# Seven block products for the second product of experts 3 to 6, and scatters of one expert that do not wait for one another

## The chip, the cores and the metric

The kernel runs on one core of a Trainium2 chip. The core has five engines with queues of their own: PE (TensorE, matrix products; its weight loads are listed apart as PEld), DVE (VectorE), ACT (ScalarE), POOL (GpSimd, which also issues the indirect DMAs) and SP (SyncE, which only issues DMAs here). Each engine works through its own instructions in order and waits on semaphores for the others. The time is that of one execution on the device in microseconds (us); the figure given is the median of several.

## The reference, cut to what matters

The whole network is four layers on 4096 tokens of width 256, all in 32-bit floats: a gated attention layer, a low-rank feed-forward layer, a 16-head attention with relu weights, and a mixture of experts. The change is in the last one:

```python
S = sigmoid(xt @ Wg).T              # 8 experts x 4096 tokens
G, I = top_k(S, 1024)               # each expert takes its 1024 best tokens
ex = xt[I]                          # gathered rows
hid = gelu(einsum('ekh,ehf->ekf', ex, W1) + b1)       # 256 -> 1024
out = (einsum('ekf,efh->ekh', hid, W2) + b2) * G      # 1024 -> 256
new_x = zeros_like(xt).at[I].add(out)                 # scattered back, added
```

Then `new_x` is normalized by rows and added to `x`. The tokens of one expert are distinct; two experts may take the same token, so a row of `new_x` may be added to by several experts.

## The kernel before, in words

Experts are worked on one after another, 0 to 7 (`e`). An expert's 1024 tokens are two units of 512 (`u = 2e` and `2e + 1`, `q` is 0 or 1), each of four tiles of 128 tokens.

*Lists.* For each expert a threshold is searched and the list of its tokens is built by small steps on DVE, PE and ACT (`sort`, `rank`, `chunks`, `places`, `collect`, `gather`). These steps stand in an agenda, and `go_on_with_lists(u, time)` (L2357), called after pieces of the main work, takes the next step when the time credited since the last one suffices and the step is due at unit `u`. The list of expert `e` is due from unit 2e - 3 on, its gather from 2e - 2. The gather (L2003 to L2012) is eight indirect DMAs issued by POOL that fetch rows of tokens into `got`.

*Turning.* `turn` (L2167) transposes four tiles of gathered rows on PE into a PSUM bank and copies them to `xT`, the layout that the first product wants. `turns_within` (L2209) says after which tile of the second product of the expert before this is done.

*First product.* Experts 0, 1, 2 and 7 use `feed_forward` (L2275). Experts 3 to 6 use `feed_forward_by_seven` (L2225): a 2 x 2 block product in the form of Winograd, with seven block products in place of eight. Its token sums T1, T2, T3, T4 are made on DVE (`token_sums`, L2202), its weight sums S1 to S4 on POOL (`weight_sums`, L2190). For each of four `f` it makes seven matmuls of 128 x 512 into four PSUM banks a, b, c, d, adds them up on DVE and applies gelu on ACT into `hid`.

*Second product.* `project_back` (L2307): for each tile of 128 tokens, eight matmuls (one for each 128 of the 1024 hidden features) of 256 columns accumulate in one PSUM tile `py` (tag "y", two buffers). DVE adds the bias (L2331) and multiplies by the gates (L2332) into `y`, and POOL adds the rows to `acc_d` in memory by an indirect DMA with addition (L2333). The hidden block is the stationary operand (128 x 128), the weights `w2` are the moving one.

*Order of scatters.* Every scatter writes `acc_d`, so each waits until the one before has landed. For expert 6 alone they are declared independent of one another (L2342 to L2344); they are collected in `summed`.

*Expert 7.* Its result is not scattered. When expert 6's scatters have landed, SP reads blocks of 512 rows of `acc_d` back (`read_back`, L2053) and POOL fetches the rows of expert 7's own tokens (`fetch_acc`, L2084). Then, between the matmuls of expert 7, the steps of `beside_last` (L2134) run: statistics of a block on DVE and POOL (`all_stats`), scaling on ACT (`all_scaled`), addition to the output (`all_out`, on POOL's queue for blocks 0 to 4, DVE and SP for 5 to 7), and the same for expert 7's own rows (`known`, `chosen_stats`, `chosen_less_mean`, `chosen_sum`, `chosen_out`). Keys such as `(0, "f", 6)` mean: in unit q = 0, after feature block 6 of the first product; `"i"` means after tile i of the second.

*What sets the order.* PE, DVE and ACT run in the order in which the program is written (`manual_schedule`). POOL's order is planned by the framework's scheduler up to expert 5, and is the written one from expert 6 on (L2391). SP issues loads in order. PSUM has eight banks: one for `parts`, five with tag "mm", two for tag "y"; a tag's buffers are used in turn, and one that is used again waits until its last reader is done.

Of the kernel before, what the change touches and what calls it, by code (L numbers as in the profile page):

```python
# [9 lines left out]
F32 = mybir.dt.float32  # L10
# [4 lines left out]
ALU = mybir.AluOpType  # L15
# [4 lines left out]
P = 128  # L20
# [54 lines left out]
def kernel(  # L75
# [1679 lines left out]
    with ExitStack() as st4:  # L1755
# [364 lines left out]
        def begin_last():  # L2120
# [45 lines left out]

        def turn(u, c, half=None):  # L2167

# [3 lines left out]
            tiles = range(NJ) if half is None else range(half * NJ // 2, (half + 1) * NJ // 2)  # L2172
            tp = ps.tile([P, NJ, P], F32, tag="mm", name="tp", bufs=5)
            for i in tiles:
# [34 lines left out]
        def turns_within(u):  # L2209

            e, q = divmod(u, QPE)
            if u == QPE * NE - 1:
                return {}
            turns = {c: (lambda c=c: turn(u + 1, c)) for c in range(DC)}
            if q == QPE - 1 and by_seven(e + 1):
                both = [
                    turns[0], turns[1], lambda: turn(u + 2, 0), lambda: token_sums(e + 1, 0), lambda: turn(u + 2, 1),
                    *(lambda n=n: token_sums(e + 1, n) for n in (1, 2, 3)),
                ]
                return {0: both[0:1], 1: both[1:4], 2: both[4:]}  # L2220
            if by_seven(e) and q == 0:
                return {}
            return {2: [turns[0], turns[1]]} if u == 1 else {1: [turns[0]], 2: [turns[1]]}

        def feed_forward_by_seven(e):  # L2225
# [81 lines left out]
        def project_back(u, hid):  # L2307
# [4 lines left out]
            for i in range(NJ):  # L2312
                k = q * NJ + i
                py = ps.tile([P, D], F32, tag="y", name="py")
                for f in range(FC):
# [14 lines left out]
                y = wk.tile([P, D], F32, tag="y", name="y", bufs=7)  # L2330
                nc.vector.tensor_tensor(y, py, mb2[:, e, :], ALU.add)  # L2331
# [102 lines left out]
```

## Time and profile before

| | |
|---|---|
| median of 3 runs | 1458.32 us (1456.48 to 1459.18) |
| profiled execution | 1456.37 us, of which the span from first to last instruction is 1454.2 us |
| PE busy in the span | 1405.7 us, 97% |
| DVE, ACT, POOL busy | 869.7, 735.8, 531.7 us |
| granted PE clock | 0.985 of full, on average |
| expert 3 starts (first matmul of its first product) | 1169.2 us |
| experts 4, 5, 6, 7 start | 1224.2, 1279.3, 1334.3, 1388.4 us |
| last matmul | about 1444 us |

A row of the chain of work reads: start, length, engine, output tile, line, and how many records it merges. A 32-bit matmul leaves two records. A row of the timeline of one engine reads: start, length, engine, line, operation, output <- input, shape; in brackets the idle time of that engine before it and what ended it. A row of the table by stage reads: start:end, length, and for PE, PEld, DVE, ACT and POOL the busy time with the number of instructions, then the granted PE clock, the DMA share and GB/s.

### The profile page before, as it was taken

Reading aid. Unit: us, or ns where it says so; the run is one execution under the profiler, and the core shown is the slowest. Engines: PE = TensorE matmul, PEld = TensorE weight load, DVE = VectorE, ACT = ScalarE, POOL = GpSimd, SP = SyncE. Lnnn points to the kernel's source line nnn. Section 1 sums busy time; section 2 is a strip of 40 time slices with the busy share of each in tenths; the row PEclk is TensorE's granted clock in tenths of the full one; section 3 lists DMA queues with packets and bytes.
Section 4 is the critical chain, followed back from the end, with each engine's and each line's share of the span. In section 5 each row is a group of like instructions: output and inputs, shape, how many; then the busy total and the mean of one; then the engine's idle time right before and its main releaser. Section 6 shows DMA issues by size and latency. Waiting matters only on the chain.

```text
span 1454.2 us, 26447 instructions
## 1 busy us (share of the span) xinstructions
PE 1405.7 (97%) x10392; PEld 858.6 (59%) x10392; DVE 869.7 (60%) x2133; ACT 735.8 (51%) x1014; POOL 531.7 (37%) x662
## 2 busy tenths in 40 slices
PE   8999999999889999999999999949999999999997
PEld 4666666666644444454444547727666657757774
DVE  5457555666554637664767496885545766365346
ACT  4244454454358887877787888712122131231243
POOL 4123322322352223422333323413425325543765
PEclk9999999999999999999999999979999999999999
DMA  8400000001652473437344721151414233343364
GB/s 223 142 1 1 0 1 1 1 1 38 203 173 76 122 209 104 143 118 232 91 133 144 229 70 39 39 170 38 106 19 127 51 79 70 78 103 62 81 166 134
DMA packets 104853, 138.76 MB, mean 95 GB/s; under 512 B 25469, under 2 KB 64794, under 8 KB 104602
## 3 DMA queue, kind: packets, MB, share of 16 engines
q1 hardware_dynamic: 74512, 81.75, 18.1%
q0 software_dynamic: 30160, 55.32, 16.1%
q8 instruction: 81, 1.33, 0.4%
q14 instruction: 42, 0.34, 0.1%
q10 hardware_dynamic: 58, 0.01, 0.0%
HBM read 75.29 MB, written 61.51 MB: 94 GB/s over the span
## 4 chain that ended last, share of the span: by engine, by line
PE 87%; DVE 5%; issue 3%; POOL 2%; DMA 1%; ACT 1%; SPq 0%; POOLq 0%; ACTq 0%; DVEq 0%
PE po L1553 16%; PE py L2316 14%; PE sc L1532 10%; PE ph L2290 7%; PE ph L2236 7%; PE pg L722 4%; PE pv L738 4%; PE py L848 3%; PE pt L1308 2%; PE pq L397 2%; PE po L820 2%; PE ph L904 2%; PE pv L431 2%; PE po L824 1%; PE pkv L835 1%
## 5 line engine op out<-in xcount | busy, mean ns | idle before, releaser
L1710 ACT ACTIVATE w<-sc 128x1024 f32<-128x1024 f32 x395 | 379.9, 1023 | 60.7 <-PE sc L1532 60.2
L1553 PE MATMUL po<-w,vaug 128*17 128x256 f32 (+1 forms) x4608 | 256.0, 358 | 1.5 <-DVE turned L1611 1.2
L2316 PE MATMUL py<-w,hid 128*128 128x256 f32 x1024 | 228.6, 380 | 0.0
L2316 PEld LDWEIGHTS py<-w,hid 128*128 128x128 f32 x1024 | 191.9, 190 | 29.6 <-issue 4.2
L1712 DVE TENSOR_SCALAR w<-sc 128x1024 f32<-128x1024 f32 x117 | 142.4, 1220 | 79.4 <-PE sc L1532 75.9
L1553 PEld LDWEIGHTS po<-w,vaug 128*17 128x17 f32 x4608 | 116.3, 97 | 117.9 <-issue 48.2
L1532 PE MATMUL sc<-q,kT 64*128 64x512 f32 (+1 forms) x1152 | 170.3, 403 | 2.5 <-ACT w L1710 1.3
L2333 POOL DMA_INDIRECT acc_d<-y,idx x56 | 88.6, 1583 | 163.0 <-issue 38.6
L1532 PEld LDWEIGHTS sc<-q,kT 64*128 64x128 f32 x1152 | 90.1, 185 | 83.5 <-issue 46.6
L2297 ACT ACTIVATE hid<-ph,mb 128x512 f32<-128x512 f32 (+1 forms) x72 | 46.0, 639 | 159.6 <-PE ph L2290 133.3
L2290 PE MATMUL ph<-xT,w 128*128 128x512 f32 (+1 forms) x288 | 114.8, 552 | 0.3 <-DVE xT L2181 0.3
L2005 POOL DMA_INDIRECT got<-tok_d,idx x64 | 66.6, 1040 | 72.1 <-DVE idx L1995 54.1
L2290 PEld LDWEIGHTS ph<-xT,w 128*128 128x128 f32 x288 | 52.6, 190 | 51.3 <-issue 48.3
L371 POOL DMA_DIRECT2D kT<-k_d x32 | 23.4, 732 | 118.0 <-PE sc L1532 54.0
L722 PE MATMUL pg<-nT,wh 128*128 128x512 f32 x128 | 61.6, 613 | 1.5 <-ACT nT L661 1.5
L2331 DVE TENSOR_TENSOR y<-py,mb 128x256 f32<-128x256 f32 x56 | 23.5, 420 | 64.3 <-PE py L2316 54.9
L848 PE MATMUL py<-wo,oT 128*128 128x256 f32 x256 | 61.6, 384 | 0.0
L738 PE MATMUL pv<-wh,nT 128*128 128x512 f32 x128 | 59.7, 593 | 0.0
L848 PEld LDWEIGHTS py<-wo,oT 128*128 128x128 f32 x256 | 47.5, 190 | 17.6 <-issue 11.1
L746 ACT ACTIVATE v<-v 128x512 f32<-128x512 f32 x32 | 20.2, 630 | 62.7 <-DVE v L745 62.7
L1137 POOL TENSOR_TENSOR rsb<-veb,mhalf 128x1 f32<-128x1 f32 x30 | 19.6, 654 | 86.8 <-DVE veb L1136 86.8
L586 POOL TENSOR_TENSOR x<-x,y 128x1024 f32<-128x1024 f32 x13 | 30.6, 2357 | 56.3 <-ACT y L575 56.3
(352 smaller groups left out, 2344.8 us busy)
## 6 DMA issues: line engine op xcount, KB each, us to landing
q<-q_d POOLq DMA_DIRECT2D x16, 1024.0 KB, 6.0
kT<-k_d POOLq DMA_DIRECT2D x32, 512.0 KB, 8.1
w<-in_L_ffn_W_dram SPq DMA_DIRECT2D x16, 1024.0 KB
k_d<-parts SPq DMA_DIRECT2D x48, 256.0 KB
q_d<-parts SPq DMA_DIRECT2D x48, 256.0 KB
acc_d<-logits SPq DMA_DIRECT2D x8, 512.0 KB
tok_d<-hg SPq DMA_DIRECT2D x30, 128.0 KB
x<-in_L_attn_x_dram SPq DMA_DIRECT2D x7, 512.0 KB
```

Source lines behind the costliest of these rows:

```text
L722: nc.tensor.matmul(pg, lhsT=wh[:, c, HID + e * P : HID + (e + 1) * P], rhs=d["nT"][:, c, :], start=(c == 0), stop=(c == DC - 1),)
L738: nc.tensor.matmul(pv, lhsT=d["nT"][:, c, i * P : (i + 1) * P], rhs=wh[:, c, 0:HID], start=(c == 0), stop=(c == DC - 1),)
L848: nc.tensor.matmul(py, lhsT=d["oT"][:, e, :], rhs=wo[:, e, :], start=(e == 0), stop=(e == EC - 1))
L1532: nc.tensor.matmul(sc[:, j, m * n : (m + 1) * n], lhsT=row["kT"][t, r][rows, u, (kt + m) * P : (kt + m + 1) * P], rhs=row["q"][qh, t][rows ...
L1553: nc.tensor.matmul(po[rows : rows + HD + 1, at : at + n], lhsT=row["v"][:, kt + m, HQ * t + 4 * r + 2 * u + j, :], rhs=w[:, j, (2 * m + pa ...
L1710: nc.scalar.activation(w, sc, AF.Relu)
L1712: nc.vector.tensor_scalar(w, sc, 0.0, None, ALU.max)
L2005: return nc.gpsimd.indirect_dma_start(out=dst, out_offset=None, in_=rows[:, :], in_offset=self.at_chunk(c), bounds_check=NT - 1, oob_is_er ...
L2236: nc.tensor.matmul(bank, lhsT=a[:, f * P : (f + 1) * P], rhs=b, start=start, stop=stop, skip_group_check=not start)
L2290: nc.tensor.matmul(ph, lhsT=w1[:, c, f * P : (f + 1) * P], rhs=xT[u][:, c, h * n : (h + 1) * n], start=(c == 0), stop=(c == DC - 1),)
L2316: nc.tensor.matmul(py, lhsT=hid[:, f, i * P : (i + 1) * P], rhs=w2[:, f, :], start=(f == 0), stop=(f == FC - 1),)
L2333: scatter = nc.gpsimd.indirect_dma_start(out=acc_d[:, :], out_offset=lists[e].at_chunk(k), in_=y, in_offset=None, bounds_check=NT - 1, oob ...
```

## The change

It has four parts.

1. The second product of experts 3 to 6 no longer goes through `project_back` but through a new function, `project_back_by_seven`. The hidden activations (1024 tokens x 1024 features) are cut in 2 x 2 blocks of 512 x 512, the weights in 2 x 2 blocks of 512 x 128. Four weight sums are made on POOL (`back_sums`, emitted after the first `f` of the first product), four sums of hidden blocks on DVE, and seven block products of 16 matmuls each (128 columns) replace the eight. Rooms of weights that are no longer used (`wq1`, `wk1`, `wv`, `wop`) and `accg` hold the sums; the others are made in place. The bias times the gate is written by ACT, the gated sums are added on DVE by blocks of 128 x 128. All eight scatters of an expert come after the sixth and seventh block product.
2. The scatters of one expert are declared independent of one another for every expert, and each waits for all scatters of the expert before.
3. Within experts 3 to 6 the transposes for the next expert use the PSUM tag "y", which the new second product leaves free; `py` tiles become a whole bank each, and `y` gets nine buffers in place of seven.
4. In expert 7 the statistics of the blocks move one step later.

```diff
+        scattered = [*([] for _ in range(NE - 2)), summed]
...
         beside_last = {
-            (0, "f", 5): [(all_stats, 0)],
-            (0, "f", 6): [(all_stats, 1)],
-            (0, "f", 7): [(all_scaled, 0), (known, 0), (all_stats, 2), (fetch_acc, 4, 5)],
-            (0, "i", 0): [(all_out, 0), (all_scaled, 1), (known, 1), (all_stats, 3)],
-            (0, "i", 1): [(all_out, 1), (all_scaled, 2), (known, 2), (all_stats, 4), (fetch_acc, 6, 7)],
-            (0, "i", 2): [(all_out, 2), (all_scaled, 3), (known, 3)],
-            (0, "i", 3): [(all_out, 3), (all_scaled, 4), (all_stats, 5)],
-            (1, "f", 0): [(all_out, 4)],
+            (0, "f", 6): [(all_stats, 0)],
+            (0, "f", 7): [(all_stats, 1), (all_scaled, 0), (known, 0), (fetch_acc, 4, 5)],
+            (0, "i", 0): [(all_out, 0), (all_scaled, 1), (known, 1), (all_stats, 2)],
+            (0, "i", 1): [(all_out, 1), (all_scaled, 2), (known, 2), (all_stats, 3), (fetch_acc, 6, 7)],
+            (0, "i", 2): [(all_out, 2), (all_scaled, 3), (known, 3), (all_stats, 4)],
+            (0, "i", 3): [(all_out, 3), (all_scaled, 4)],
+            (1, "f", 0): [(all_out, 4), (all_stats, 5)],
...
+        def turn(u, c, half=None, tag="mm"):
...
+            tp = ps.tile([P, NJ, P], F32, tag=tag, name="tp", bufs=5 if tag == "mm" else 2)
...
+            tag = "y" if by_seven(e) else "mm"
...
+                if f == 0:
+                    back_sums(e, gelus[-1])
                 go_on_with_lists(QPE * e, 3.0)
-            for q in range(QPE):
-                if q == 0 and by_seven(e + 1):
-                    weight_sums(e + 1, gelus[-1])
-                if q == 0 and e == NE - 2:
-                    fetch_last()
-                project_back(QPE * e + q, hid[q])
+            if by_seven(e + 1):
+                weight_sums(e + 1, gelus[-1])
+            if e == NE - 2:
+                fetch_last()
+            project_back_by_seven(e, hid)
...
+        def back_sums(e, behind):
+            (b11, b12), (b21, b22) = back_blocks(e)
+            t1, t2, t4 = (room.rearrange("p (f n) -> p f n", n=P) for room in back_rooms[:3])
+            for dst, x, y in ((t1, b12, b11), (t2, b22, t1), (b12, b22, b12), (t4, b21, t2)):
+                after_all(nc.gpsimd.tensor_tensor(dst, x, y, ALU.subtract), [behind])
...
+            def product(bank, a, b, start, stop):
+                for i in range(NJ):
+                    for f in range(HC):
+                        nc.tensor.matmul(
+                            bank[:, i * P : (i + 1) * P],
+                            lhsT=a[:, f, i * P : (i + 1) * P],
+                            rhs=b[:, f, :],
...
+            def of_bias(q):
+                for k in range(q * NJ, (q + 1) * NJ):
+                    ys[k] = wk.tile([P, D], F32, tag="y", name="y", bufs=9)
+                    nc.scalar.activation(ys[k], mb2[:, e, :], AF.Identity, scale=gates[k])
+            def add(q, n, src):
+                for i in range(NJ):
+                    k = q * NJ + i
+                    y = ys[k][:, n * P : (n + 1) * P]
+                    nc.vector.scalar_tensor_tensor(y, src[:, i * P : (i + 1) * P], gates[k], y, ALU.mult, ALU.add)
+            def put(q):
+                for k in range(q * NJ, (q + 1) * NJ):
+                    scatter = nc.gpsimd.indirect_dma_start(
...
+                    after_all(scatter, scattered[e - 1] if e else ())
+                    beside_each_other(scatter, scattered[e])
...
+            p1 = new_bank("p1")
+            product(p1, a11, b11, True, True)
+            nc.scalar.copy(u2, p1)
+            nc.vector.tensor_tensor(s1, a21, a22, plus)
+            nc.vector.tensor_tensor(s3, a11, a21, sub)
+            go_on_with_lists(QPE * e, 1.2)
+            p4 = new_bank("p4")
+            product(p4, a22, t4, True, True)
+            nc.vector.tensor_tensor(s2, s1, a11, sub)
+            go_on_with_lists(QPE * e, 1.2)
+            product(p1, a12, b21, False, True)
+            of_bias(0)
+            add(0, 0, p1)
+            nc.vector.tensor_tensor(s4, a12, s2, sub)
+            go_on_with_lists(QPE * e, 1.2)
+            for do in ahead.get(0, ()):
+                do()
+            p5 = new_bank("p5")
+            product(p5, s1, t1, True, True)
+            nc.scalar.copy(kept, p5)
+            for do in ahead.get(1, ()):
+                do()
+            go_on_with_lists(QPE * e + 1, 1.2)
+            p6 = new_bank("p6")
+            product(p6, s2, t2, True, True)
+            nc.vector.tensor_tensor(u2, u2, p6, plus)
+            of_bias(1)
+            for do in ahead.get(2, ()):
+                do()
+            go_on_with_lists(QPE * e + 1, 1.2)
+            p7 = new_bank("p7")
+            product(p7, s3, t3, True, True)
+            nc.vector.tensor_tensor(v, u2, p7, plus)
+            nc.vector.tensor_tensor(c21, v, p4, plus)
+            nc.vector.tensor_tensor(v, v, kept, plus)
+            add(1, 0, c21)
+            add(1, 1, v)
+            put(1)
+            go_on_with_lists(QPE * e + 1, 1.2)
+            product(p5, s4, b22, False, True)
+            nc.vector.tensor_tensor(u2, u2, p5, plus)
+            add(0, 1, u2)
+            put(0)
+            go_on_with_lists(QPE * e + 1, 1.2)
...
-                if e == NE - 2:
-                    beside_each_other(scatter, summed)
+                after_all(scatter, scattered[e - 1] if e else ())
+                beside_each_other(scatter, scattered[e])
```

In `project_back_by_seven`, `a11`, `a12` are the two feature halves of the first unit's hidden block and `a21`, `a22` those of the second; `s1` is a room of its own (`accg`), `s2`, `s3`, `s4` overwrite `a11`, `a21`, `a12`.

More of the change, by code (lines that the diff above doesn't have):

```diff
@@ L2165 @@
         xT = {}
-        def turn(u, c, half=None):
+        def turn(u, c, half=None, tag="mm"):
             if c == 0 and not half:
@@ L2172, in turn @@
             tiles = range(NJ) if half is None else range(half * NJ // 2, (half + 1) * NJ // 2)
-            tp = ps.tile([P, NJ, P], F32, tag="mm", name="tp", bufs=5)
+            tp = ps.tile([P, NJ, P], F32, tag=tag, name="tp", bufs=5 if tag == "mm" else 2)
             for i in tiles:
@@ L2213, in turns_within @@
                 return {}
-            turns = {c: (lambda c=c: turn(u + 1, c)) for c in range(DC)}
+            tag = "y" if by_seven(e) else "mm"
+            turns = {c: (lambda c=c: turn(u + 1, c, tag=tag)) for c in range(DC)}
             if q == QPE - 1 and by_seven(e + 1):
                 both = [
-                    turns[0], turns[1], lambda: turn(u + 2, 0), lambda: token_sums(e + 1, 0), lambda: turn(u + 2, 1),
+                    turns[0], turns[1], lambda: turn(u + 2, 0, tag=tag), lambda: token_sums(e + 1, 0),
+                    lambda: turn(u + 2, 1, tag=tag),
                     *(lambda n=n: token_sums(e + 1, n) for n in (1, 2, 3)),
@@ new lines, in feed_forward_by_seven, with back_blocks @@
+            project_back_by_seven(e, hid)
+        back_rooms = [x.rearrange("p c d -> p (c d)") for x in (wq1, wk1, wv, wop)]
+        def back_blocks(e):
+            w2 = weights[e][1]
+            return [[w2[:, h * FC // 2 : (h + 1) * FC // 2, n * P : (n + 1) * P] for n in range(2)] for h in range(2)]
+        def back_sums(e, behind):
[3 more added lines that the diff above has]
+                after_all(nc.gpsimd.tensor_tensor(dst, x, y, ALU.subtract), [behind])
@@ new lines, in project_back_by_seven, with new_bank @@
+        def project_back_by_seven(e, hid):
+            (b11, t3), (b21, b22) = back_blocks(e)
+            t1, t2, t4 = (room.rearrange("p (f n) -> p f n", n=P) for room in back_rooms[:3])
+            HC = FC // 2
+            (a11, a12), (a21, a22) = ([hid[q][:, h * HC : (h + 1) * HC, :] for h in range(2)] for q in range(QPE))
+            s1 = accg.rearrange("p k d -> p (k d)").rearrange("p (f t) -> p f t", t=TB)
+            s2, s3, s4 = a11, a21, a12
+            u2, v, c21 = back_rooms[3], seven["sum1"], seven["sum0"]
+            ahead = turns_within(QPE * e + 1)
+            gates = [lists[e].got[k][:, D + e : D + e + 1] for k in range(NC)]
+            ys = {}
+            kept = wk.tile([P, TB], F32, tag="kept_back", name="kept_back", bufs=1)
+            def new_bank(name):
+                return ps.tile([P, TB], F32, tag="mm", name=name, bufs=5)
+            def product(bank, a, b, start, stop):
[5 more added lines that the diff above has]
+                            rhs=b[:, f, :],
+                            start=start and not i and not f,
+                            stop=stop and f == HC - 1,
+                            skip_group_check=True,
+                        )
+            def of_bias(q):
[10 more added lines that the diff above has]
+                    scatter = nc.gpsimd.indirect_dma_start(
+                        out=acc_d[:, :],
+                        out_offset=lists[e].at_chunk(k),
+                        in_=ys[k],
+                        in_offset=None,
+                        bounds_check=NT - 1,
+                        oob_is_err=True,
+                        compute_op=ALU.add,
+                    )
+                    after_all(scatter, scattered[e - 1] if e else ())
+                    beside_each_other(scatter, scattered[e])
+            sub, plus = ALU.subtract, ALU.add
+            p1 = new_bank("p1")
[42 more added lines that the diff above has]
+            go_on_with_lists(QPE * e + 1, 1.2)
@@ L2313, in project_back @@
                 k = q * NJ + i
-                py = ps.tile([P, D], F32, tag="y", name="py")
+                py = ps.tile([P, TB], F32, tag="y", name="py")[:, 0:D]
                 for f in range(FC):
@@ L2329, in project_back @@
                     continue
-                y = wk.tile([P, D], F32, tag="y", name="y", bufs=7)
+                y = wk.tile([P, D], F32, tag="y", name="y", bufs=9)
                 nc.vector.tensor_tensor(y, py, mb2[:, e, :], ALU.add)
```

## The prediction

> **What bounds the kernel now.** I read the page's head first, then engine busy time cut by stage, then the chain that ended last inside the expert stage.
>
> ```profile
> span 1454.2 us, 26447 instructions
> PE 1405.7 (97%) x10392; PEld 858.6 (59%) x10392; DVE 869.7 (60%) x2133; ACT 735.8 (51%) x1014; POOL 531.7 (37%) x662
> ...
> 1224.20:1279.30 55.10, 55.10 (x237) 37.33 (x236) 28.72 (x61) 15.41 (x25) 26.66 (x22) 1.00 0.37 80
> ...
> 1388.40:1454.20 65.80, 55.93 (x200) 36.89 (x198) 38.01 (x140) 26.57 (x48) 37.61 (x43) 0.96 0.61 164
> ```
>
> The first row below the dots is expert 4 (start, end, length; then busy us of PE, PEld, DVE, ACT, POOL; granted clock; DMA). PE is busy for all 55.10 us at full clock, so in experts 3 to 6 time is PE time. The last row is expert 7 with the finish: 56 of 65.8 us are PE, and what follows the last matmul is fixed. The chain through expert 4's second product shows no other engine:
>
> ```profile
> 1249.77 17.27 PE py L2316 x80
> 1267.03 0.44 PE tp L2175 x4
> 1267.47 3.46 PE py L2316 x16
> 1270.92 0.87 PE tp L2175 x8
> 1271.80 0.06 PE parts L1907 x2
> 1271.86 3.54 PE py L2316 x16
> 1275.39 0.44 PE tp L2175 x4
> 1275.83 3.46 PE py L2316 x16
> ```
>
> A matmul is two records, so 128 records are 64 matmuls of 256 columns: 17.27 + 3.46 + 3.54 + 3.46 = 27.73 us, 0.433 each. There is no wait in it to spare.
>
> **Product: 64 matmuls of 256 columns become 7 x 16 = 112 of 128 columns.** Such a shape runs in the first layer, eight in a row in the chain:
>
> ```profile
> 79.87 0.22 PE po L820 x2
> 80.09 0.22 PE po L824 x2
> ...
> 81.43 0.22 PE po L824 x2
> 81.66 0.89 PE psim L688 x8
> ```
>
> 81.66 - 79.87 = 1.79 us for eight, 0.224 each: 3.58 per block product, 25.06 per expert, 2.67 less than now, **10.7 us less for four experts**. Half of 0.433 would give 24.3 and 13.9 saved; I take the row, since the shape is the same.
>
> Here a rule speaks against the change. The same row's weight loads take 192 ns each (224 of them) but are busy 34.0 us together, not 43: they overlap one another. The Trainium skill, "TensorE: Matmul & The Clock Gate", section "Back-to-back issue gap", says that in a stream of weight load and matmul pairs both set the spacing: 81 ns for 128 columns against 56 for the matmul alone. That ratio on 0.217 gives 0.314 per matmul, 35.2 us per expert, 7.4 more than now. The eight in the trace keep their pace, so I stay with 0.224 (0.217 to 0.235 for a run of 112).
>
> **Order within an expert.** From T, the end of the first product, PE does p1 to T+3.6, p4 to 7.2, p1's second half to 10.7, four transposes, p5 to 14.8, eight transposes, p6 to 19.2, four, p7 to 23.2, p5's second half to 26.8. The token sums have 2048 elements a partition; a 512-element one costs DVE 0.60 start to start, so 2.2 each. The last gelu ends at T+1.5 (as now), so S1 is ready at 3.8 (first needed at 11.2), S3 at 6.0 (19.6), S2 at 8.2 (15.6); S4 waits for the adds of p1 and is ready at 14.1 (23.2). All hidden, with 7 us or more to spare. ACT's bias rows (eight of 0.5) and two copies of 0.6 hide too. The weight sums of the second product are four POOL subtractions of 1.3, needed when p4 starts, 28 us after the expert's start.
>
> **A new wait at the next expert's start.** Behind p6 DVE has three token sums (ready 22.2 after T) and the ranking of the list after next, 1.85 (as at 1175.84), so v begins at 24.0, not 23.2. Then v 0.8, c21 and v 0.6 each, eight gated adds of 0.27 [...], u2 0.8, four adds, chunks 1.0: 31.1. Only then come the next expert's own sums. Its third matmul wants p5's bank at 28.5 and gets it at 28.9; its sixth wants its C22 sum to have been read, 32.6, at 31.1. After that it catches up. I price this at **1.5 us for each of experts 4, 5 and 6: 4.5** (bounds 0.5 and 2.5 each).
>
> **Expert 3 alone** finds POOL free, so its four subtractions run in the first product, where DVE ranks and builds chunks. A DVE tensor_scalar beside such POOL work waits now:
>
> ```profile
> 1205.57 1.92 DVE L2332 TENSOR_SCALAR y<-y,got 128x256 f32<-128x256 f32 x1
> 1209.03 2.78 DVE L2332 TENSOR_SCALAR y<-y,got 128x256 f32<-128x256 f32 x1
> ```
>
> Its usual time is 0.35. The Trainium skill, "SBUF — State Buffer", section "SBUF: two separate sides", calls the port that DVE and GpSimd share an exclusive lock and counts DVE operations with two SBUF inputs as well. By it S1 to S4 could lose another 5.3 us to the next expert's weight sums on POOL; the slack above takes that, so both readings cost nothing there. In expert 3, two blocked tensor_scalars of up to 2.4 each against 0.45 us of slack: **1.5** (0 to 3.5).
>
> **Scatters.** In experts 0 to 5 one scatter waits for the last (1160.78, 1165.49, 1169.87: 4.6 apart, of which 1.9 are work). PE never waits for them, so independence itself is worth nothing before expert 6; without it, though, eight scatters that all come at an expert's end would take 37 us. Now they take eight times 1.87, 15 us. In experts 4 to 6 the four weight sums queue behind them: 15.4 to 20.7 after the start, before the gathers that are ready at 18.7 and finish at 31.2. First needs: p4 at 28, the turns at 35. Hidden, with 7 and 4 us.
>
> **Expert 7: where the gain goes.** Now expert 6's scatters spread over its second product and the last starts 1.1 us after expert 7's start (1388.36). In the change none can start before p7's sums: v, c21, v and five adds after p7, about at expert 7's start. Seven times 1.87 later the last begins: +13.1, **12 us later relative to expert 7**. Everything of expert 7 that reads the sums hangs on it:
>
> ```profile
> 1389.48 1.55 POOL L2333 DMA_INDIRECT acc_d<-y,idx  x1 [1.32 <-DVE y L2332]
> 1394.10 1.08 POOL L2005 DMA_INDIRECT accg<-acc_d,idx  x1 [3.06 <-DMA acc_d<-y,idx]
> ...
> 1396.71 1.41 DVE L2046 BATCH_NORM_STATS2 stc<-back_w 128x6 f32<-128x256 f32 x4 [7.50 <-DMA back_w<-acc_d]
> ...
> 1418.60 0.69 ACT L2297 ACTIVATE hid<-ph,mb 128x512 f32<-128x512 f32 x1 [2.27 <-PE ph L2290]
> ```
>
> Fetch 4.62 and statistics 7.23 after the last scatter: +17.7 and +20.3 (now +5.7 and +8.4). DVE then does two statistics (1.87 each) and one known (0.4) before it frees the first py bank, +25.0; PE has done its two tiles and four transposes at +21.1 and waits 3.9 us. The statistics now one step later in the order keep this from being 1.9 more. POOL next: four fetches 5.1, five scale pairs of 1.35, four more fetches 5.2, three stores of 1.0, so the scale of block 4 comes 20.9 after the first fetch (now 19.9), +38.6. ACT scales block 4 (2.0) ahead of the second half's first gelu, which now waits for PE with 2.3 to spare. Then eight gelus of 0.6 and six half scalings of 1.0, with 1.2 lost to block 5: the last gelu ends at +52.3 and PE's first tile at +52.8, now +45.6. **Slip 7.2**; the eighth store and the scatters of the result, 1.35 each, then run POOL bound: **8.5 in all** (6 to 11).
>
> **Sum.** -10.7 + 4.5 + 1.5 + 8.5 = +3.8: span 1454.2 to 1458.0. Around it lie 2.2 us in the profiled execution (1456.37), which itself stands 1.95 under the median of 1458.32; so a median of **1462**, 0.26% slower. The measurement tells about 0.2% (2.9 us) from no change.
>
> **Rivals.**
> *The tail is paid by PE's wait alone*: ACT catches up, the transitions cost 0.5 each, expert 3 nothing: -10.7 + 1.5 + 3.9 = -5.3, **1453**. For it: ACT is busy 26.6 of 65.8 us. Against it: the order on ACT is fixed, scaling before gelu. 0.15.
> *Weight loads bind at 128 columns*: +7.4 per expert, with the tail but no transition waits, +30 + 8.5: **1497**. For it the rule above, against it the row. 0.04.
> *POOL takes the gathers before the weight sums* (its order is planned, not written, up to expert 5; the sums are then ready at 31 to 32, p4 waits about 3.5): at three experts 10.5 more, **1472**. It decides as soon as the sums start later than 23 us into an expert. Against it: they come earlier in the program. 0.13.
> *The forecast*, 0.68, own range 1456 to 1468; about 0.4 of it lies within 0.2%.
>
> So faster 0.15, same 0.27, slower 0.58. Range 1454 to 1473: it leaves out the better half of the first rival and the loads, and reaches to the queue on POOL; rates of 0.217 or 0.235 move the sum by -3 or +5, inside it.
>
> **What would show it.** The second product at about 25 us per expert (112 matmuls, 0.224 apart); PEld without idle time; PE waits of 1 to 2 us on DVE in the first six matmuls of experts 4 to 6; the last scatter of expert 6 starting 12 to 14 us after expert 7's first matmul; PE waiting for accg at its third py tile, ACT's gelus of the second half behind a scaling. Wrong if the tail's slip is under 5 us, if matmuls of 128 columns drift apart over a long run, or if p4 waits for POOL.

## The result, and the profile after

The changed kernel takes 1468.37 us (median of 5 runs, 1465.1 to 1471.38) beside 1459.18 us for the kernel before (5 runs, 1456.48 to 1460.06): a ratio of 1.0061 with a 95% interval of 1.0049 to 1.0073, 9 us slower. The forecast was slower by 0.26%, 1462 us. Measured a second time in a later batch of runs, the ratio was 1.0065 (1.0048 to 1.0082). Batches stand on different chips, on which the kernel before had medians from 1455 to 1460 us, so below I compare ratios, or the lengths of stages in the traces.

The head of the page after has PE busy for 7.8 us less than before:

```profile
span 1463.3 us, 27377 instructions
PE 1397.9 (96%) x10776; PEld 863.1 (59%) x10776; DVE 910.3 (62%) x2169; ACT 753.5 (51%) x1054; POOL 575.5 (39%) x678
```

The span is 9.1 us longer all the same, so PE must stand idle somewhere. The table by stage shows where. Its rows are experts 3, 5 and 7 (the last with the finish); the columns are as before.

```profile
1166.00:1225.70 59.70, 54.88 (x334) 38.88 (x333) 42.73 (x74) 19.86 (x35) 26.75 (x18) 0.97 0.21 58
1279.40:1333.10 53.70, 52.53 (x332) 38.06 (x332) 38.46 (x70) 19.76 (x35) 37.30 (x24) 1.00 0.37 79
1385.80:1463.30 77.50, 59.05 (x201) 38.40 (x199) 39.93 (x147) 26.35 (x48) 47.79 (x50) 0.90 0.61 149
```

Expert 5 lasts 53.7 us instead of 55.0, so the product does save. Expert 3 lasts 59.7 instead of 55.0, with a granted clock of 0.97 instead of full, and expert 7 with the finish 77.5 instead of 65.8, with a clock of 0.90 and 18 us in which PE is not busy (9.9 before). From expert 3's start to the end, the two profiled executions stand 285.0 to 297.3 us: +4.6 in expert 3, -1.3 in each of experts 4, 5 and 6, +11.7 from expert 7 on. (That is 12.3, and the span grew by 9.1: expert 3 began 3.2 us earlier in the changed kernel's execution, 1166.0 against 1169.2. In the kernels below, whose work up to there is that of the change, its start lay between 1165.6 and 1168.8. The 3.2 us stand there already in the second half of expert 0, and experts 1 and 2 last equally long, so I take them for a difference of the execution, which is not shown.)

The chain of waits through expert 4's second product, to be read beside the chain of before:

```profile
1252.49 10.72 PE p L2312 x96
1263.21 0.44 PE tp L2175 x4
1263.64 3.57 PE p L2312 x32
1267.22 0.87 PE tp L2175 x8
1268.09 3.57 PE p L2312 x32
1271.66 0.45 PE tp L2175 x4
```

Three block products take 10.72 us and one 3.57: 0.223 us for each matmul of 128 columns, with no gap between these rows.

### The profile page after: what moved, and what is told of

It is laid out like the page before. It is cut to its first block, busy times and chain, and to the rows that moved or that the text cites. A ratio compares the mean times of both kernels' runs of the same rounds, so it can differ in the third digit from the quotient of the medians.

```text
span 1463.3 us, 27377 instructions
## 1 busy us (share of the span) xinstructions
PE 1397.9 (96%) x10776; PEld 863.1 (59%) x10776; DVE 910.3 (62%) x2169; ACT 753.5 (51%) x1054; POOL 575.5 (39%) x678
## 4 chain that ended last, share of the span: by engine, by line
PE 84%; DVE 8%; issue 3%; POOL 2%; ACT 1%; DMA 1%; POOLq 0%; DVEq 0%; SPq 0%; ACTq 0%
PE po L1553 15%; PE sc L1532 10%; PE py L2433 6%; PE ph L2238 6%; PE ph L2407 6%; PE p L2312 5%; PE pg L722 4%; PE py L848 4%; PE pv L738 4%; PE ph L904 2%; PE pq L397 2%; PE po L820 2%; PE pt L1308 2%; PE pv L431 2%; PE pk L397 2%
## 5 line engine op out<-in xcount | busy, mean ns | idle before, releaser
L2433 PE MATMUL py<-w,hid 128*128 128x256 f32 x512 | 118.2, 387 | 7.0 <-DVE accg L2444 6.0
L2005 POOL DMA_INDIRECT got<-tok_d,idx x64 | 84.3, 1317 | 76.7 <-DVE idx L1995 59.6
L2433 PEld LDWEIGHTS py<-w,hid 128*128 128x128 f32 x512 | 97.0, 193 | 24.0 <-DVE accg L2444 6.3
L738 PE MATMUL pv<-wh,nT 128*128 128x512 f32 x128 | 59.7, 592 | 0.0
L2312 PE MATMUL p<-w,hid 128*128 128x128 f32 x512 | 59.4, 276 | 0.0
L2312 PEld LDWEIGHTS p<-w,hid 128*128 128x128 f32 x512 | 58.4, 192 | 1.8 <-issue 1.8
```

Of the source, the lines that this page charges most:

```text
L738: nc.tensor.matmul(pv, lhsT=d["nT"][:, c, i * P : (i + 1) * P], rhs=wh[:, c, 0:HID], start=(c == 0), stop=(c == DC - 1),)
L2005: return nc.gpsimd.indirect_dma_start(out=dst, out_offset=None, in_=rows[:, :], in_offset=self.at_chunk(c), bounds_check=NT - 1, oob_is_er ...
L2312: nc.tensor.matmul(bank[:, i * P : (i + 1) * P], lhsT=a[:, f, i * P : (i + 1) * P], rhs=b[:, f, :], start=start and not i and not f, stop= ...
L2433: nc.tensor.matmul(py, lhsT=hid[:, f, i * P : (i + 1) * P], rhs=w2[:, f, :], start=(f == 0), stop=(f == FC - 1),)
```

## The experiments

All lengths by stage, in us, with the ratio of each kernel to the kernel before. The last two columns are the start of POOL's first fetch of accg after expert 7's first matmul, and the time from that fetch to the end of the span. The stages come from one traced execution of each kernel; two of the same kernel, the change, differ by 1.8 us in the last stage and by 0.1 in the others.

| kernel | exp. 3 | 4 | 5 | 6 | 7 to end | ratio (95%) | fetch | fetch to end |
|---|---|---|---|---|---|---|---|---|
| before | 55.0 | 55.0 | 55.0 | 54.0 | 65.8 | 1 | 5.7 | 60.1 |
| the change | 59.7 | 53.7 | 53.7 | 52.7 | 77.5 | 1.0061 (1.0049 to 1.0073) | 18.7 | 58.8 |
| the change again | 59.8 | 53.7 | 53.7 | 52.7 | 79.3 | 1.0065 (1.0048 to 1.0082) | 18.6 | 60.6 |
| scatters_alone | 55.0 | 55.1 | 55.0 | 58.4 | 65.8 | 0.9998 (0.9989 to 1.0008) | 5.7 | 60.1 |
| six_as_before | 59.7 | 53.7 | 53.7 | 60.9 | 70.1 | 1.0053 (1.0037 to 1.0068) | 5.8 | 64.3 |
| three_sums_late | 55.3 | 53.7 | 53.7 | 52.7 | 80.1 | 1.0037 (1.0024 to 1.0050) | 18.7 | 61.4 |
| stats5_back | 59.7 | 53.7 | 53.7 | 52.7 | 76.5 | 1.0058 (1.0042 to 1.0075) | 18.8 | 57.7 |
| three_no_hidden_sums | 59.3 | 53.7 | 53.7 | 52.7 | 79.6 | 1.0086 (1.0072 to 1.0101) | 18.5 | 61.0 |
| stats_not_moved | 59.8 | 53.7 | 53.7 | 52.7 | 77.4 | 1.0086 (1.0068 to 1.0105) | 18.5 | 58.9 |
| seven_clock_held | 58.1 | 53.7 | 53.7 | 52.7 | 79.6 | 1.0112 (1.0094 to 1.0130) | 18.4 | 61.2 |
| six_front_first | 62.5 | 53.7 | 53.7 | 52.7 | 75.1 | 1.0062 (1.0049 to 1.0075) | 16.0 | 59.1 |
| three_to_five_best | 54.1 | 52.7 | 52.7 | 61.2 | 67.2 | 0.9988 (0.9980 to 0.9995) | 5.9 | 61.3 |
| four_five_best | 55.0 | 52.4 | 52.8 | 60.1 | 65.8 | 0.9989 (0.9979 to 0.9998) | 5.8 | 60.0 |
| landed_known | 54.0 | 52.7 | 52.7 | 60.5 | 67.4 | 0.9982 (0.9975 to 0.9990) | 5.7 | 61.7 |

### The scatters alone

The scatters of one expert are independent, everything else is as before but for nine buffers for y and a whole bank for each `py`.

```diff
+        def back_by_seven(e):
+
+            return False
...
-            tag = "y" if by_seven(e) else "mm"
+            tag = "y" if back_by_seven(e) else "mm"
...
-            project_back_by_seven(e, hid)
+            if back_by_seven(e):
+                project_back_by_seven(e, hid)
+            else:
+                for q in range(QPE):
+                    project_back(QPE * e + q, hid[q])
```

> The second product of all experts as before, statistics of expert 7 in the old order; only the scatters of one expert are independent, and py tiles and y buffers as in the change. Theory (PE sets the pace, nothing on it waits for a scatter before expert 6): within 1.5 us of before, 1459. Rival (the independent scatters themselves disturb gathers or DMA): slower by 3 us or more; or faster by 2 us or more if POOL's queue had been on the path.

1459.99 us beside 1460.3: no difference, as the prediction had it ("independence itself is worth nothing before expert 6"). But its trace shows a wait that nobody forecast, in expert 6. The timeline of DVE:

```profile
1370.46 0.42 DVE L2457 TENSOR_TENSOR y<-py,mb 128x256 f32<-128x256 f32 x1 [8.19 <-remote]
```

DVE's second y of expert 6 stands for 8.19 us behind something that the profile names only "remote", PE in turn waits 2.61 us for a free bank, and the expert lasts 58.4 us instead of 54.0. This comes back below.

### Expert 6 as before, experts 3 to 5 changed

The edit is that of scatters_alone, with another answer in `back_by_seven`, and the statistics stay as in the change.

```diff
+        def back_by_seven(e):
+
+            return 3 <= e < 6
```

> The change, but expert 6 takes the old second product, so that its scatters spread again. Theory (late scatters of expert 6 cost 11.7 us in expert 7, expert 6 itself won 1.3): 10 us less than the change, about 1458; the last scatter starts 1 to 2 us after expert 7's first matmul and PE does not wait for accg. Rival (expert 7 is slow because its statistics were moved): expert 7 stays 8 us or more longer than before, 1467.

1468.21 us, a ratio of 1.0053, so the expectation failed. Two things took the gain. Expert 6 has the wait just seen (7.75 and 4.73 us "remote") and lasts 60.9 us. And expert 7 lasts 70.1 us although the scatters are early again and the fetch comes at +5.8:

```profile
1396.30:1466.40 70.10, 56.54 (x201) 36.78 (x199) 37.93 (x140) 26.25 (x48) 36.85 (x43) 0.94 0.58 154
```

That is 4.3 us more than before. What is left of the change in this stage is the order of the statistics, one step later than before. The kernels that have early scatters and the old order lie at 65.8 to 67.4 us, so by one trace of each the moved statistics cost 2.7 to 4.3 us when the scatters are early.

### Expert 3's weight sums later

The four POOL sums of expert 3 go out behind the third group of its first product instead of the first.

```diff
-                if f == 0:
+                if f == (2 if e == 3 else 0):
                     back_sums(e, gelus[-1])
```

> The change, but expert 3 issues the weight sums of its second product after the third block of the first product, not after the first, when DVE no longer ranks. Theory (POOL subtractions block DVE's ranking, PE waits 2.5 us for C22 and its clock then halves): expert 3 loses neither, about 4 us less than the change, 1464; the granted clock stays at 1.00 in expert 3's first product. Rival (the ranking alone is too long): no gain, 1468, the wait stays.

1465.22 us, ratio 1.0037 beside 1.0053 and 1.0058 of the two kernels of the same batch that have expert 3 as in the change. Expert 3's row, and DVE's operation that had been held up:

```profile
1166.90:1222.20 55.30, 53.06 (x335) 38.29 (x334) 39.64 (x74) 19.63 (x35) 26.73 (x18) 1.00 0.21 63
```

```profile
1174.66 0.19 DVE L1928 TENSOR_TENSOR chosen<-chosen,kinds 128x32 f32<-128x32 f32 x1
```

0.19 us again instead of 1.17, full clock, and 55.3 us instead of 59.7: in the trace the theory held. The ratio is lower by 0.0016 and 0.0021, some 2.3 and 3.1 us, but the intervals overlap.

### Block 5's statistics back by a step

```diff
-            (0, "i", 3): [(all_out, 3), (all_scaled, 4)],
-            (1, "f", 0): [(all_out, 4), (all_stats, 5)],
+            (0, "i", 3): [(all_out, 3), (all_scaled, 4), (all_stats, 5)],
+            (1, "f", 0): [(all_out, 4)],
```

> The change, but the statistics of block 5 stand where they stood before, ahead of the store of block 4. Theory (POOL's order makes ACT wait 2.3 us for block 5's scale): 1 to 1.5 us less than the change, 1467. Rival (the end is bound by PE's late tiles or by the scatters of the result, not by this scale): no change within 0.5 us, or slower since DVE frees py later.

1468.54 us, ratio 1.0058, no gain. ACT's wait of 2.30 us for block 5's scale is gone from its timeline, but one of 0.78 us for block 6 takes its place, and the stage is 1.0 us shorter, less than two traces of the change differ by.

### Expert 3 without the sums of hidden rows

```diff
-            nc.vector.tensor_tensor(s1, a21, a22, plus)
-            nc.vector.tensor_tensor(s3, a11, a21, sub)
+            if e == 3:
+                s1 = a21
+            else:
+                nc.vector.tensor_tensor(s1, a21, a22, plus)
+                nc.vector.tensor_tensor(s3, a11, a21, sub)
```

and likewise for the other two. So this kernel leaves out work that the result needs.

> In expert 3 the four sums of hidden rows (S1 to S4, four additions of 128x2048 on DVE, 2.29 us each) are left out and the products take the rows unsummed, so this kernel's output is not the reference's. Theory: these sums stretch POOL's gathers of got in expert 3, from 1.01 us to 2.0 to 2.8 us each, so the turn of expert 3's end waits about 3 us for got. Without them the four gathers take 1.0 us each again, the wait at the turn is gone, and expert 3 lasts 56.5 to 57 us where the changed kernel's lasts 59.7: 1465.3 us. Rival: the gathers are late only because POOL's four weight sums stand ahead of the lists' steps in its queue; then the gathers start as late as before, and the wait at the turn stays over 1.5 us: 1467 to 1468.5.

The time missed: 1468.06 us, ratio 1.0086. The mechanism did not. POOL's timeline and the row of expert 3's second product (30.15 us from 1195.55 to 1225.70 in the change):

```profile
1203.48 1.01 POOL L2005 DMA_INDIRECT got<-tok_d,idx  x1 [0.30 <-issue]
```

```profile
1199.50:1226.60 27.10, 27.10 (x245) 27.09 (x244) 9.98 (x30) 7.95 (x16) 13.28 (x12) 1.00 0.26 80
```

All eight gathers take 1.0 to 1.1 us, PE does not wait for got, and the second product is 3.05 us shorter. POOL stood idle for 20.7 us between the weight sums and the first gather, so the rival (the queue) is out. In the trace, what hid the gain is the first product, 32.1 us here against 29.55 in the change: this time four of DVE's operations were held up and PE waited 3.67 us, not 2.51.

### The statistics in their old order

The order of the statistics of before, everything else as in the change.

```diff
-            (0, "f", 6): [(all_stats, 0)],
-            (0, "f", 7): [(all_stats, 1), (all_scaled, 0), (known, 0), (fetch_acc, 4, 5)],
+            (0, "f", 5): [(all_stats, 0)],
+            (0, "f", 6): [(all_stats, 1)],
+            (0, "f", 7): [(all_scaled, 0), (known, 0), (all_stats, 2), (fetch_acc, 4, 5)],
...
```

> Only the order of the statistics beside expert 7 goes back to that of the kernel before; everything else is the changed kernel. The prediction's claim: with the late scatters the statistics one step later keep the end from being 1.9 us more, so 1470.3 us. Rival: the statistics wait for the same fetch of accg whichever step they are put in, and only the engine that waits changes; DVE is reached by the fetch at +18.7 us either way, so 1468.4 within 1 us. Second rival, from the kernel whose sixth expert kept its old second product (its end was 4.3 us longer than before although its scatters were spread out): the move itself puts block 5's scaling on POOL behind the output of block 4 and costs, so 1465 to 1467.

Expert 7 to the end is 77.4 us, the change's 77.5 and 79.3. In its batch the ratio, 1.0086, is that of three_no_hidden_sums; the change itself was not in that batch. The timeline of PE:

```profile
1417.62 5.33 PE L2434 MATMUL py<-w,hid 128*128 128x256 f32 x16 [7.79 <-DVE accg L2445]
```

PE waits 7.79 us at its third tile instead of 6.02, 1.8 more, very nearly the 1.9 of the prediction. The end does not move with it (77.4 us beside 77.5 and 79.3). So the price of the wait was right, and to add it to the end was wrong.

### The clock held beside expert 7's wait

26 matmuls in bf16 on an idle bank, ahead of the third tile.

```diff
+                if u == QPE * (NE - 1) and i == 2:
+                    keep_busy(ps.tile([P, TB], F32, tag="mm", name="idle7", bufs=5), 26)
                 py = ps.tile([P, TB], F32, tag="y", name="py")[:, 0:D]
```

> 26 bf16 matmuls on an idle bank are put ahead of the third tile of expert 7's first second product, so that PE does not stand idle for 6 us there; nothing else is changed. Theory: the granted clock stays at 1.0 in the tiles after the wait (they take 3.6 us instead of up to 6.0), PE is some 3.5 us further on, but the end is set by ACT and POOL behind the scalings of blocks 4 and 5, so no more than 1 us comes of it: 1467.5 to 1468.5 us. Rival: PE's own chain sets the end, and the 3.5 us come back: 1465 us.

PE's timeline shows the third tile at its usual pace:

```profile
1411.07 3.72 PE L2435 MATMUL py<-w,hid 128*128 128x256 f32 x16 [0.55 <-DVE accg L2446]
```

3.72 us instead of 5.98, and the first half of expert 7 is 34.9 us long instead of 37.0. The second half then is 44.7 instead of 40.5: 79.6 in all, ratio 1.0112. PE waits for ACT's gelus five times there, not twice. The rival (PE's own chain, and so the halved clock, sets the end) is out: what PE gained came to nothing at the end. Whether the kernel got slower by it is not shown, since its interval overlaps those of its batch and the change itself was not in that batch.

### Expert 6's front half first

The products in the order p1, p4, p1, p5, p6, p5, p7, in expert 6 alone, the first four scatters ahead of p7. The later calls for the lists' steps are left out there.

```diff
+                product(p5, s4, b22, False, True)
+                nc.vector.tensor_tensor(v, u2, p5, plus)
+                add(0, 1, v)
+                put(0)
...
+                p7 = new_bank("p7")
+                product(p7, s3, t3, True, True)
...
+                put(1)
```

> In expert 6 alone the seven products are put in another order: those of the first half of the tokens end first, its four scatters go out before the seventh product, and the last four follow tile by tile. Theory: the last scatter's issue comes some 6 to 7 us earlier (about 7.5 us after expert 7's first matmul instead of 14.1), the fetch of accg and all behind it with it, PE no longer waits 6 us at the third tile, and the end is about 6 us earlier: 1462.5 us. Rival: something else than the scatters' lateness holds the end (the moved statistics, POOL behind block 4's output); then 1466 or more.

1464.3 us, ratio 1.0062, the lowest of its batch by 3 us but not the 6 hoped for. POOL's timeline, and the row of expert 7:

```profile
1399.93 1.56 POOL L2334 DMA_INDIRECT acc_d<-y,idx  x1 [0.30 <-ACT hid L2458]
```

```profile
1388.60:1463.70 75.10, 58.50 (x200) 37.87 (x199) 41.45 (x149) 26.36 (x48) 46.76 (x49) 0.94 0.63 154
```

The last scatter starts 11.3 us after expert 7's first matmul, 2.8 earlier than in the change: the first one went out only 2.1 us ahead of expert 7, and eight in a row take 15 us. The fetch comes 2.7 us earlier and the stage is 2.4 us shorter (4.2 against the other trace of the change). So the end follows the scatters here too, as far as single traces tell; my estimate of how early they could go was wrong.

### Experts 3 to 5 or 4 and 5 alone, and the change again

Three edits follow from this: the old second product in expert 6 with the old order of the statistics; expert 3's weight sums late and its gathers one step earlier; and the last call of the list's steps at an expert's end left out, since DVE's chunks (1.12 us) stand there ahead of the next expert's first C22. There are 12 buffers for y, and in expert 6 the list may go on one step earlier. four_five_best has the same, with expert 3 as in the kernel before.

```diff
-                    go_on_with_lists(QPE * e, 3.2, True)
+                    go_on_with_lists(QPE * e, 3.2, e < NE - 2 or f != 1)
+                elif e == 3:
+                    go_on_with_lists(QPE * e, 3.2)
...
             add(0, 1, u2)
             put(0)
-            go_on_with_lists(QPE * e + 1, 1.2)
```

> The changed kernel itself once more, beside the two versions below and under the same runs of the kernel before: 9 us above the kernel before, as in its first measurement. The wait of PE at expert 3's sixth matmul is 2.5 or 3.7 us (three or four of DVE's small operations held up beside POOL's weight sums), and expert 3 lasts 58 to 62.5 us.

1468.51 us, ratio 1.0065, with the wait of 2.51 us in expert 3.

> Seven products in the second product of experts 3, 4 and 5 alone; expert 6 keeps the old second product with its scatters spread over it, and the statistics beside expert 7 stand where they stood before. Expert 3's weight sums go out three steps later and its gathers one step earlier; the last call of the list's steps at the end of each expert's second product is left out, so that no step's DVE work stands ahead of the next expert's first C22; expert 6's list may be collected one step earlier; and there are 12 buffers for y instead of 9, so that no y of expert 6 waits for the scatter just before it. Theory: experts 3, 4, 5 last 53.7, 52.6, 52.6 us, expert 6 53 to 54, expert 7 to the end 65.8 as before: 6 to 7 us less than the kernel before, about 1452. Rival: expert 6's gathers still come too late, its scatters back up behind them as in the kernel whose expert 6 alone kept the old product (60.9 us), and the gain is spent: no better than the kernel before.

> The same with seven products in the second product of experts 4 and 5 alone, and expert 3 as in the kernel before (55.0 us). Theory: experts 4 and 5 53.7 and 52.6 us, expert 6 53 to 54: 4 us less than the kernel before. If expert 3's gathers beside DVE's sums still cost PE its wait for got in the version with expert 3, this one is the faster of the two.

1457.02 us (ratio 0.9988) and 1456.87 us (0.9989): both a little faster than the kernel before (1.2 and 1.4 us, with intervals that end just below 1), in the same batch in which the change is 0.65% slower. Experts 3 to 5 of the first (rows of experts 3, 4, 6 and 7):

```profile
1166.70:1220.80 54.10, 52.69 (x335) 38.34 (x334) 39.69 (x74) 19.63 (x35) 26.79 (x18) 1.00 0.23 64
1220.80:1273.50 52.70, 52.52 (x333) 38.08 (x332) 38.28 (x70) 19.63 (x35) 36.62 (x24) 1.00 0.37 82
1326.20:1387.40 61.20, 56.14 (x227) 37.23 (x226) 26.36 (x54) 13.12 (x21) 39.77 (x31) 0.97 0.44 83
1387.40:1454.60 67.20, 56.00 (x201) 36.95 (x199) 38.12 (x140) 26.90 (x48) 38.86 (x43) 0.93 0.60 161
```

54.1, 52.7 and 52.7 (expert 5, by the table) are within 0.4 us of what the theory asked for. PE's timeline at the start of expert 5 has the wait for C22 down from 1.17 us to 0.18:

```profile
1277.99 1.13 PE L2243 MATMUL ph<-x,w 128*128 128x512 f32 x2 [0.18 <-DVE hid L2260]
```

Expert 6 keeps its 61.2 us, as the rival said (four_five_best: 60.1), and eats most of the gain. The last run went after that wait; in it the list of expert 7 may also be gathered half a step earlier.

```diff
                 y = wk.tile([P, D], F32, tag="y", name="y", bufs=12)
-                nc.vector.tensor_tensor(y, py, mb2[:, e, :], ALU.add)
+                added = nc.vector.tensor_tensor(y, py, mb2[:, e, :], ALU.add)
+                if e == NE - 2:
+                    after_all(added, [scattered[e - 1][k]])
```

> The version with seven products in experts 3 to 5, with two edits in expert 6: every y there waits first for the landing of one of expert 5's scatters, which is long past (so its waits have the form they have in the kernel before, where the landing of a later scatter of the same queue stands ahead of y, and no wait for got stands between y and its scaling), and the list of expert 7 may be gathered half a step earlier. Theory: the 7.0 and 5.6 us for which DVE's y stood behind no releaser that the profile names come of the form of these waits; they are gone, expert 6 lasts 54 us instead of 61.2, and the whole is about 1450, 0.5% below the kernel before. Rival: they come of POOL's row of transfers itself, and stay: expert 6 at 58 us or more, and 1455 to 1457.

1456.68 us, ratio 0.9982 (0.9975 to 0.9990): the lowest ratio of all, though the intervals overlap, and 2.4 us under the kernel before in its batch. But the theory of the wait fell. DVE's timeline in expert 6:

```profile
1370.48 0.42 DVE L2458 TENSOR_TENSOR y<-py,mb 128x256 f32<-128x256 f32 x1 [8.37 <-issue]
```

A wait of 8.37 us again, which the profile now puts down to nothing at all. Expert 6 lasts 60.5 us.

## Why the prediction was right, and where its size was off

The side was right (slower), and the time lies in the range (1454 to 1473). The size is off: +3.8 us forecast, about +9 measured. That the range held is in part luck: the forecast's own range, 1456 to 1468, was just missed, and the wide one reached up to 1473 for a queue on POOL that did not come. Two terms lie outside the bounds that they were given: expert 3's loss (1.5 us forecast, 0 to 3.5; measured 4.6 + 2.67 = 7.3) and the slip of the tail (8.5, 6 to 11; measured 11.7).

**The product: right.** Forecast -2.67 us an expert at 0.224 us a matmul; measured 0.223 over a run of 96 records. The rule of the Trainium skill that I had set against it ("TensorE: Matmul & The Clock Gate", "Back-to-back issue gap": 81 ns with weight loads against 56 without, at 128 columns) would have made 0.314 of it, an estimate by its ratio. It doesn't carry over to these two-record 32-bit matmuls, and the rival of 1497 us falls with it. POOL did take the weight sums ahead of the gathers (the rival of 1472 us is out too).

**The wait at the next expert's start: right.** Forecast 1.5 us each for experts 4 to 6; measured 1.17 to 1.18 at the sixth matmul. Experts 4, 5 and 6 came to -1.3 us each against a forecast of -1.2. It is DVE's doing: without the chunks at the expert's end the wait is 0.18 (three_to_five_best). PE's timeline in expert 4 of the change:

```profile
1231.13 1.12 PE L2238 MATMUL ph<-x,w 128*128 128x512 f32 x2 [1.18 <-DVE hid L2255]
```

**Expert 3: the step that failed most.** Forecast -2.67 + 1.5 = -1.2 us, measured +4.6. There are two causes, one mis-sized and one denied. The timelines of POOL, DVE and PE in its first product:

```profile
1173.55 1.26 POOL L2290 TENSOR_TENSOR wq<-w 128x512 f32<-128x512 f32 x1 [4.07 <-ACT hid L2243]
1174.89 1.32 POOL L2290 TENSOR_TENSOR wk<-w,wq 128x512 f32<-128x512 f32 x1
...
1173.69 1.17 DVE L1928 TENSOR_TENSOR chosen<-chosen,kinds 128x32 f32<-128x32 f32 x1
1174.89 0.19 DVE L1931 SCALAR_TENSOR_TENSOR place<-place,chosen 128x32 f32<-128x32 f32 x1
1175.12 1.13 DVE L1933 TENSOR_SCALAR hi<-place 128x32 f32<-128x32 f32 x1
1176.28 1.20 DVE L1935 SCALAR_TENSOR_TENSOR lo<-hi,place 128x32 bf16<-128x32 f32 x1
...
1178.92 2.08 PE L2238 MATMUL ph<-x,w 128*128 128x512 f32 x2 [2.51 <-DVE hid L2255]
```

Three small DVE operations (0.19 us otherwise) each last until one of POOL's four sums is done, 2.9 us longer together, where I had two blocked tensor_scalars. They are not tensor_scalars alone: two of them have two SBUF inputs, which the Trainium skill ("SBUF — State Buffer", "SBUF: two separate sides") counts in, and which I had priced only for S1 to S4. PE then waits 2.51 us, inside my bound of 3.5. What no step had is the next row, the table by stage just behind that wait:

```profile
1178.90:1181.50 2.60, 2.58 (x3) 1.18 (x4) 2.11 (x5) 0.72 (x1) 0.00 (x0) 0.50 0.00 0
```

The granted clock is 0.50, and four matmul records take 3.33 us from 1178.92 on, where they take 1.72 at full clock: 1.6 us on top. Moving the sums away (three_sums_late) removes 4.4 us in one stroke, wait and clock together.

The second cause lies in the second product, where I wrote that both readings of the shared port "cost nothing there", since the slack took S1 to S4's delay. I had looked at what POOL does to DVE, and not at what DVE does to POOL:

```profile
1196.77 1.11 POOL L2005 DMA_INDIRECT got<-tok_d,idx  x1 [18.11 <-DVE idx L1995]
1198.18 2.26 POOL L2005 DMA_INDIRECT got<-tok_d,idx  x1 [0.30 <-issue]
1200.74 1.97 POOL L2005 DMA_INDIRECT got<-tok_d,idx  x1 [0.30 <-issue]
1203.01 2.09 POOL L2005 DMA_INDIRECT got<-tok_d,idx  x1 [0.30 <-issue]
...
1197.20 2.29 DVE L2350 TENSOR_TENSOR accg<-hid 128x2048 f32<-128x2048 f32 x1 [0.71 <-ACT hid L2243]
1199.53 2.29 DVE L2351 TENSOR_TENSOR hid<-hid 128x2048 f32<-128x2048 f32 x1
...
1212.71 0.33 PE L2175 MATMUL tp<-ident,got 128*128 128x128 f32 x1 [1.22 <-DMA got<-tok_d,idx]
1214.04 0.33 PE L2175 MATMUL tp<-ident,got 128*128 128x128 f32 x1 [1.00 <-DMA got<-tok_d,idx]
```

Gathers of 1.01 us last 2 to 2.8 us beside DVE's four sums of 2.29 us; each of the four ends 0.9 to 1.0 us after one of the sums (1199.49 and 1200.44, 1201.82 and 1202.71). The row is 5.1 us late, and PE waits at the turn. In expert 5 the gathers start 21.8 us after the expert's start (I had 20.7), and the same stretching is hidden. In expert 3 they start only 30.8 us after the expert's start. Leaving the sums out took 3.05 us off the second product, so this cause is shown.

**Expert 7: right in mechanism, 3.2 us short.** Forecast +8.5, measured +11.7 (the second trace: +13.5). The steps in order, after expert 7's first matmul, forecast and measured: last scatter +13.1 and +14.1; fetch +17.7 and +18.7; statistics +20.3 and +21.4; PE's wait at the third tile 3.9 and 6.02; block 4 scaled +38.6 and +40.0; last gelu's end +52.3 and +55.0; then the scatters of the result, slip 8.5 and 11.7. The timelines of POOL, DVE, PE and ACT:

```profile
1399.90 1.56 POOL L2334 DMA_INDIRECT acc_d<-y,idx  x1 [0.30 <-issue]
1404.54 1.09 POOL L2005 DMA_INDIRECT accg<-acc_d,idx  x1 [3.08 <-DMA acc_d<-y,idx]
...
1407.19 1.41 DVE L2047 BATCH_NORM_STATS2 stc<-back_w 128x6 f32<-128x256 f32 x4 [18.61 <-DMA back_w<-acc_d]
...
1412.91 5.98 PE L2433 MATMUL py<-w,hid 128*128 128x256 f32 x16 [6.02 <-DVE accg L2444]
...
1425.81 2.07 ACT L2071 ACTIVATE back<-back,msc,rsc 128x256 f32<-128x256 f32 x4 [3.46 <-POOL msc L2065]
1431.33 1.09 ACT L2071 ACTIVATE back<-back,msc,rsc 128x256 f32<-128x256 f32 x2 [2.30 <-POOL msc L2065]
1440.09 0.68 ACT L2414 ACTIVATE hid<-ph,mb 128x512 f32<-128x512 f32 x1
```

The cause is the scatters: scatters_alone and stats_not_moved have the same work and order in this stage, and only the scatters come early or late; the stage lasts 65.8 and 77.4 us. The term that was mis-sized is the slack: I let 12 us of lateness become 8.5. The last column of the table says there is hardly any. The fetch-to-end time is 57.7 to 61.7 us in every kernel but one, whether the fetch is at +5.7, +16 or +18.7, and the kernel before with its 60.1 lies in the middle of it; 13.0 us of a later fetch gave 11.7 us of a later end. What ends last did change. In the kernel before, the chain of work runs through PE until the middle of expert 7 (first row), in the change it comes from expert 6's last scatter and the reading back (the other rows):

```profile
1416.78 5.16 PE ph L2290 x12
...
1399.90 3.82 DMA acc_d<-y,idx
1403.87 2.94 DMA back_w<-acc_d
```

So before the change PE and the work behind the fetch needed nearly the same time (60.1 us from the fetch to the end before, where PE sets the end; 58.8 and 60.6 after, where the fetch does). The halved clock after PE's 6 us (0.50 again) costs nothing here, since seven_clock_held removed it without a gain. ACT's wait for block 5 is worth about 1.0 us of the stage by its one trace (stats5_back).

"The statistics now one step later keep this from being 1.9 more" is refuted: in their old order the end is the same. With early scatters the move even costs 2.7 to 4.3 us (six_as_before, one trace).

**What stays open.** In expert 6's old second product, DVE's y waits (once to three times, 2 to 8.4 us each) in every kernel here that has it except the kernel before. The first one or two sums of expert 6 come on time; the next ones wait while POOL issues the gathers of xg and the first scatters. It was there with 9 buffers for y and with 12, and with the waits ordered as in the kernel before. So neither of these was shown to be the cause, and I have no other. The traces tell one thing more than the names "remote" and "issue": eight of the nine waits end 0.02 us after PE raises the semaphore on which y waits, and PE raises it 3 to 8 us after the recorded end of the tile's last matmul, where in the kernel before it takes 0.02 us at most. DVE waits for PE's signal, then; why that comes late (the profile models the ends of matmuls) is not shown. Nor is it known whether the kernel before is free of this in other executions, since one was traced. Without it, three_to_five_best would come to some 7 us less by its stages. Nor do I know why scatters_alone, 4.4 us longer in that expert by its trace, has the same median as the kernel before; only one execution of that one was traced.

## What to carry to other kernels

When a product is made shorter by making its results come later, follow the latest result to its reader at the end of the program: here 2.7 us saved on PE in expert 6 made the last scatter 13 us late, and the end moved by nearly all of it. Ahead of such a change, add up the work that must still follow that reader (here 60 us from the fetch); if it already reaches the end of the kernel before, no lateness is free. And keep POOL's sums away from DVE's small operations, and DVE's large sums with two SBUF inputs away from POOL's gathers: in both pairs the first held up the second here.

## What the runs showed of the hardware that was not expected

- POOL's indirect gathers, 1.01 us each, take 1.97 to 2.8 us beside DVE additions and subtractions of 128x2048 with both inputs in SBUF (2.29 us), and 1.0 to 1.1 us without them (three_no_hidden_sums).
- DVE operations of 128x32 (0.19 us) last 1.1 to 1.3 us beside POOL subtractions of 128x512 (1.3 us); three or four of them are caught, depending on the execution, so PE's wait is 2.51 or 3.67 us in the same code.
- An idle PE of 2.5 us can be enough to halve the granted clock (0.50 for 2.6 us). The Trainium skill ("TensorE: Matmul & The Clock Gate", "HAM oscillation — how this bites in real kernels") warns of gaps over about 3.4 us; here a shorter one was enough. After the same wait of 2.5 us the matmuls slowed in five traces (the change, the change again, six_as_before, stats5_back, stats_not_moved: 3.27 to 3.51 us for four records instead of 1.72) and kept nearly full pace in one (seven_clock_held: 1.82 us).
